# Rows of a third block gathered ahead of a conditional group, x of four chunks added on GpSimd, the second block table moved behind a weighing

## The chip, the cores and the metric

The kernel runs on one core of one Trainium2 chip. The metric is the device time of one execution in microseconds. The timeline and every time below count from the first instruction of the profiled execution of the kernel before.

## The reference

One adaLN transformer block over 4096 tokens of width 256, with linear attention (16 heads of 64) and a mixture of 8 experts of which each token takes two. Everything is float32.

```python
mod = (silu(c) @ wmod).reshape(...)            # sa, ca, ga, sb, cb, gb; |ga|, |gb| at least 0.25
h = layernorm(x) * (1 + ca) + sa
q, k, v = split(h @ w_qkv)                     # 16 heads of 64
q = softmax(q * 64**-0.5, axis=-1)             # over the head's columns
k = softmax(k, axis=-2)                        # over the tokens
ctx = einsum('bhnd,bhne->bhde', q, k)
x = x + ga * (einsum('bhde,bhnd->bhne', ctx, v) @ w_out + b_out)
h = layernorm(x) * (1 + cb) + sb
p = softmax(h @ Wg + bg)                       # 8 experts
sel = p on its two largest, divided by their sum (+1e-8)
e = gelu(h @ W1[e] + b1[e]) @ W2[e] + b2[e]    # hidden width 1024, each expert
x = x + gb * sum_e sel[e] * e
```

## The kernel before

The 4096 tokens are eight chunks of 512, a chunk being four tiles of 128 tokens (`TPC = 4`). Tile `t` of chunk `i` lies in `xs[i][:, t, :]`; `hT[i]` holds the normalized input of the chunk, transposed, in two blocks of 128 features (`KB = 2`).

**First half (0 to 342 us).** Keys, their column maxima, queries, the context and from it one matrix `weff` of 256 by 264, so that attention's output of a tile is two matmuls with the tile's `hT` as weights. The last 8 columns give what attention adds to the router's logits; `raw` holds the part of the logits that comes from x.

**Residual and routing (342 to 404 us).** `residual(i, half, cols)` makes two tiles of a chunk in one PSUM tile `po` of a pool of three. For each tile it issues two matmuls with `weff`, then one matmul with the identity that adds x (256 columns) and one that adds `raw` (8 columns). `products(i)` calls it for both halves; `park(i)` calls `keep`, where ScalarE copies `po` to `xs[i]` and to `logits`. `chunk_stats(i)` takes mean and variance of four tiles on VectorE (`bn_stats`, `bn_aggr`). A `Route` of a chunk makes its expert choice: `distances`, `power` (the exponential, ScalarE), `choose` (VectorE, result `both`), `places` (TensorE, result `pp`), `weigh` and `aim` (VectorE, beginning with the instructions that write `total` and `of_hot`), `mark` (8 one-hot tiles of a chunk on GpSimd and 8 on VectorE, written over parts of `hT` and `weff_t` that are no longer needed), `enlist` (8 matmuls that add the marks to the PSUM tile `listed`). Routes 0 to 3 are chunks 0 to 3; route 4, named `last`, holds chunks 4 to 7.

**Blocks (404 to 935 us).** Tokens are worked on by expert, in blocks of 256 (pairs) or 128 (single) rows of one expert. `early_table` makes the table of five blocks from the first three chunks; `late_table` makes the rest, 23 pairs and 15 singles, and needs the counts `cnt2` of all chunks. A table's `where` gives the row and expert of a block; `name_tokens` turns the lists into token numbers, `who`. For a block, `load_weights` issues two loads of 1 MB and two small ones on SyncE's queue, `load_rows` one indirect gather per 128 rows on GpSimd into one of four `held` buffers, `prepare` transposes the rows on TensorE (`ptb`) and ScalarE copies them to `xT`, `hidden` is 16 matmuls `ph` with a gelu each two, `weights_of` multiplies the gate weights (`g`, `gs`), `project` is 16 matmuls `py` for a pair and 8 for a single, then two VectorE instructions per 128 rows (the weighing, result `y`), and `add_to_out` scatters `y` into the output by GpSimd, adding, one scatter after the other. PSUM pool `ps_b`, three buffers, serves both `ptb` and `py`; `ps_a`, four buffers, serves `ph` and the small products.

`run` goes through blocks: hidden of block s, prepare of block s+1, then project of block s-1. Of eight chosen blocks the routing work is laid between these steps by the dictionary `steps`: `(b, 1)` runs after block b's `weights_of`, `(b, 2)` after the projection of the block ahead of b.

The order on the engines is the order of the calls as far as `InOrder` chains it, up to the end of the first five blocks; beyond, the tile scheduler places TensorE, VectorE, ScalarE and SyncE instructions, and GpSimd stays in call order.

Of the singles, four (`once`) run only if the number of units `left` exceeds 54, three (`twice`) only if it exceeds 58: two `tc.If` groups. In this input the first group runs and the second does not. `middle` is 17: blocks at positions 5 to 16 of `order_of` run, then the group `once`, then positions 17 to 35. In the text a block from position 17 on is called by its position: 17 is a single, 18 and 19 are pairs, 20 a single, 21 a pair. Ahead of a group's end the rows of what follows are gathered by `beyond`:

```python
            if s == len(some) - 2:
                load_ahead(beyond)
...
    run(order_of[EARLY:middle], once[:1], once + order_of[middle : middle + 2])
```

## Time and profile before

| what | us |
|---|---|
| times of 3 runs | 936.43, 936.63, 940.14 (median 936.63) |
| the profiled execution's own time | 936.49 |
| its span, first to last instruction | 934.7 |
| outside the span | 1.8 |
| TensorE matmul busy in the span | 879.8 (94%) |
| VectorE, ScalarE, GpSimd busy | 397.9, 341.6, 377.2 |
| mean granted TensorE clock | 0.977 |

The 94% of TensorE is a share of time in which a matmul is in the pipe, not a share of its peak. A row of the timeline reads: start, duration, engine, line, operation, output <- inputs, count, and in brackets how long the engine stood idle ahead of it and what ended that. A row of the chain of waits reads: start, duration, and what the program's last instruction was waiting for in that time, followed backwards.

### The profile page before, as it was taken

What the parts mean: (1) busy time and instruction counts of PE and PEld (TensorE: products, weight loads), DVE (VectorE), ACT (ScalarE), POOL (GpSimd) and SP (SyncE); (2) the same over time, 40 slices, a digit from 0 to 9 for tenths busy, and PEclk for the clock granted to TensorE, in tenths of its full rate; (3) what the DMA queues carried; (4) which work ended last, traced back from release to release, by engine and by line L of the source; (5) the groups of instructions that cost most, each with busy time, mean ns of one, the idle gap of its engine ahead of it and who ended that gap; (6) DMA issues with size and microseconds to landing.
All of it is one profiled execution on the core that took longest, in us unless ns stands there. A gap on an engine that the chain in (4) does not pass through costs nothing.

```text
span 934.7 us, 13057 instructions
## 1 busy us (share of the span) xinstructions
PE 879.8 (94%) x4747; PEld 661.7 (71%) x4747; DVE 397.9 (43%) x1014; ACT 341.6 (37%) x627; POOL 377.2 (40%) x330
## 2 busy tenths in 40 slices
PE   7979999999999889989799999999859999999996
PEld 4444444455545578878588989988759898898885
DVE  5454453798888838859831111112100111111111
ACT  4314343344444425363223333433324334333330
POOL 2000000478998803348843434342132333333242
PEclk9979999999999999999999999999979999999998
DMA  9000000232000002485878777785947877867622
GB/s 341 5 2 1 1 1 1 63 113 96 1 1 1 1 1 92 146 289 198 288 199 232 186 232 222 211 247 122 353 139 232 248 211 204 257 209 202 175 41 24
DMA packets 85077, 130.52 MB, mean 140 GB/s; under 512 B 11343, under 2 KB 66675, under 8 KB 85012
## 3 DMA queue, kind: packets, MB, share of 16 engines
q1 hardware_dynamic: 71568, 111.98, 36.2%
q0 software_dynamic: 13440, 17.69, 10.1%
q8 instruction: 39, 0.64, 0.3%
q14 instruction: 26, 0.21, 0.1%
q10 hardware_dynamic: 4, 0.00, 0.0%
HBM read 113.23 MB, written 17.47 MB: 140 GB/s over the span
## 4 chain that ended last, share of the span: by engine, by line
PE 74%; DVE 9%; issue 6%; POOL 5%; DMA 4%; ACT 1%; POOLq 0%; SPq 0%; ACTq 0%; DVEq 0%
PE ph L1220 19%; PE py L1241 17%; PE pk L292 12%; PE pq L292 10%; DMA out_dram<-y,who 3%; PE pctx L554 3%; PE po L36 2%; PE ph L36 2%; PE py L36 2%; POOL out_dram L36 1%; DVE hT L36 1%; POOL qs L36 1%; PE pa L367 1%; PE ptb L1193 1%; PE pt L196 1%
## 5 line engine op out<-in xcount | busy, mean ns | idle before, releaser
L1227 ACT ACTIVATE gl<-ph,b_sb 128x256 f32<-128x256 f32 (+1 forms) x280 | 122.2, 437 | 273.0 <-PE ph L1220 266.7
L36 POOL DMA_INDIRECT out_dram<-y,who x68 | 107.3, 1577 | 281.4 <-DVE y L1250 227.7
L1241 PE MATMUL py<-w_sb,gl 128*128 128x256 f32 x960 | 212.8, 379 | 0.0
L1220 PE MATMUL ph<-xT,w_sb 128*128 128x256 f32 (+1 forms) x1120 | 209.5, 346 | 0.5 <-ACT xT L1196 0.5
L1220 PEld LDWEIGHTS ph<-xT,w_sb 128*128 128x128 f32 x1120 | 186.6, 193 | 20.1 <-ACT xT L1196 0.7
L1241 PEld LDWEIGHTS py<-w_sb,gl 128*128 128x128 f32 x960 | 180.1, 190 | 23.1
L292 PE MATMUL pq<-wq,hT 128*128 128x512 f32 x256 | 118.3, 604 | 1.2 <-DVE qs L36 1.2
L292 PE MATMUL pk<-wk,hT 128*128 128x512 f32 x256 | 116.2, 606 | 0.3 <-ACT hT L199 0.3
L1249 DVE SCALAR_TENSOR_TENSOR y<-py,gs,gb_bc 128x256 f32<-128x256 f32 x60 | 29.0, 483 | 163.9 <-PE py L1241 157.4
L1206 DVE TENSOR_TENSOR g<-held,mine 128x16 f32<-128x16 f32 (+1 forms) x31 | 5.3, 172 | 209.4 <-DMA held<-tokens_d,who 209.4
L292 PEld LDWEIGHTS pk<-wk,hT 128*128 128x128 f32 x256 | 48.3, 194 | 60.1 <-issue 55.1
L292 PEld LDWEIGHTS pq<-wq,hT 128*128 128x128 f32 x256 | 46.0, 190 | 49.5 <-issue 45.9
L36 POOL DMA_INDIRECT held<-tokens_d,who x64 | 66.4, 1038 | 26.9 <-issue 17.2
L36 POOL TENSOR_TENSOR qs<-qs,qsum 128x1024 f32<-128x1024 f32 x30 | 58.2, 1941 | 15.6 <-DVE qsum L36 15.6
L36 DVE TENSOR_TENSOR qs<-qs,pk 128x1024 f32<-128x1024 f32 x31 | 37.8, 1220 | 62.3 <-ACT ka L453 44.1
L36 ACT ACTIVATE qs<-qs 128x1024 f32<-128x1024 f32 x32 | 33.8, 1055 | 38.2 <-DVE qs L36 38.2
L453 ACT ACTIVATE ka<-pk 128x1024 f32<-128x1024 f32 x24 | 24.6, 1023 | 57.9 <-PE pk L292 57.9
L498 POOL MEMSET qs<- 128x8 f32 x8 | 0.9, 118 | 110.3 <-PE pt L196 79.2
L36 DVE TENSOR_REDUCE qmax<-pq 128x16 f32<-128x1024 f32 x32 | 38.6, 1206 | 14.0 <-PE pq L292 13.8
L36 POOL TENSOR_TENSOR ka<-ka,nk_bc 128x1024 f32<-128x1024 f32 x18 | 42.6, 2364 | 0.0
L36 POOL TENSOR_SCALAR hT<-upward,slot 128x128 f16<-128x128 f16 x48 | 30.5, 924 | 25.6 <-DVE slot L36 13.3
L36 DVE TENSOR_TENSOR qs<-pq,qmax 128x1024 f32<-128x1024 f32 x32 | 39.2, 1225 | 3.1
(289 smaller groups left out, 995.6 us busy)
## 6 DMA issues: line engine op xcount, KB each, us to landing
w_sb<-in_L_ffn_W_dram SPq DMA_DIRECT2D x80, 1024.0 KB, 6.4
x<-in_L_attn_x_dram SPq DMA_DIRECT2D x16, 512.0 KB, 6.6
b_sb<-b_d SPq DMA_DIRECT2D x40, 128.0 KB, 5.9
tokens_d<-row SPq DMA_DIRECT2D x8, 528.0 KB, 2.9
out_dram<-x SPq DMA_DIRECT2D x8, 512.0 KB, 6.0
ka<-in_L_wmod_dram SPq DMA_DIRECT2D x3, 512.0 KB
out_dram<-y,who POOLq DMA_INDIRECT x68, 5.0
wk<-in_L_attn_w_qkv_dram SPq DMA_DIRECT2D x2, 512.0 KB, 8.1
```

Source lines behind the costliest of these rows:

```text
L36: ins = getattr(self.engine, name)(*args, **kwargs)
L196: on.pe.transpose(pt[:, t * P : (t + 1) * P], src[:, t, kb * P : (kb + 1) * P], ident)
L292: nc.tensor.matmul(pw[:, half * 512 : (half + 1) * 512], hT[i][:, kb, t * P : (t + 1) * P], w[:, kb, half * 512 : (half + 1) * 512], start ...
L367: nc.tensor.matmul(pa[32 * kb : 32 * kb + 32, :], gate_w[:, kb, :], plain(i)[:, kb, :], start=True, stop=True,)
L453: nc.scalar.activation(k_tile(n), pk, AF.Identity)
L554: nc.tensor.matmul(pctx[g][h * DH : (h + 1) * DH, j, :], ek[:, q * P + h * DH : q * P + (h + 1) * DH], qs[:, q, h * HW : (h + 1) * HW], st ...
L1193: on.pe.transpose(pt[:, j * P : (j + 1) * P], xg[:, j, kb * P : (kb + 1) * P], ident)
L1206: on.dve.tensor_tensor(g[:, :nt, :], xg[:, :nt, D : D + E], mine[:, b : b + 1, :].to_broadcast([P, nt, E]), ALU.mult,)
L1220: on.pe.matmul(ph[:, :rows], w1_sb[:, kb, hb * P : (hb + 1) * P], xT[:, kb, :rows], start=(kb == 0), stop=(kb == KB - 1),)
L1227: on.act.activation(gl[:, hb, :rows], ph[:, :rows], AF.Gelu_apprx_tanh, bias=b1_sb[:, hb : hb + 1])
L1241: on.pe.matmul(py, gl[:, hb, j * P : (j + 1) * P], w2_sb[:, hb, :], start=(hb == 0), stop=(hb == HB - 1),)
L1249: on.dve.scalar_tensor_tensor(y, py, gs[:, j : j + 1], gb_bc, ALU.mult, ALU.mult)
```

## The change

Three things. First, for chunks 4 to 7 the two identity matmuls of each tile are gone; ScalarE parks attention's part over the chunk's own `hT`, GpSimd adds it to `xs[i]` in one instruction per chunk (`add`), and one VectorE instruction adds `raw` to the logits of these 16 tiles. Second, between the blocks 1 and 2 of the early five, `late_table` changes place with the marks of chunks 6 and 7: the marks go ahead of the projection of block 1, the table behind it. Third, `beyond` gets one block more (three blocks of the positions 17 to 19 instead of two, and the third single of `twice` one step later than the other two), whose gather is issued in the last step of the group.

```diff
@@ residual
         po = ps_r.tile([P, 2, 512], FP, tag="r", name="po")
+        whole = i <= FIRST
...
-                    stop=False,
-                )
-            on.pe.matmul(po[:, z, :D], ident, xs[i][:, t, :], start=False, stop=(cols == D))
-            if cols > D:
+                    stop=(kb == KB - 1 and not whole),
+                )
+            if whole:
+                on.pe.matmul(po[:, z, :D], ident, xs[i][:, t, :], start=False, stop=(cols == D))
+            if whole and cols > D:
@@ keep
+    def parked(i: int):
+
+        return xs[i] if i <= FIRST else hT[i].rearrange("p kb (z d) -> p (kb z) d", d=D)
+
     def keep(i: int, half: int, po, more: bool = True):
-        on.act.activation(xs[i][:, 2 * half : 2 * half + 2, :], po[:, :, :D], AF.Identity)
+        on.act.activation(parked(i)[:, 2 * half : 2 * half + 2, :], po[:, :, :D], AF.Identity)
...
+    def add(i: int):
+        on.pool.tensor_tensor(xs[i], xs[i], parked(i), ALU.add)
@@ the order of the residual stage
     rows = {b: load_rows(b) for b in range(3)}
+    add(4)
+    add(5)
     for i in (6, 7):
         products(i)
         park(i)
...
     routes[3].begin_rows()
     routes[3].rows_on_pool(0)
     routes[3].choose()
+    add(6)
+    add(7)
+    tiles = slice((FIRST + 1) * TPC, NT)
+    on.dve.tensor_tensor(logits[:, tiles, :], logits[:, tiles, :], raw[:, tiles, :], ALU.add)
     for i in (4, 5, 6):
         chunk_stats(i)
@@ steps
-        (2, 1): [lambda: late.extend(late_table()), lambda: store(3), lambda: store(4)],
+        (2, 1): [
+            lambda: mark_last(2), lambda: mark_last(3), lambda: store(3), lambda: store(4)
+        ],
         (2, 2): [
-            lambda: mark_last(2), lambda: mark_last(3),
-            lambda: last.enlist(0), lambda: last.enlist(1),
+            lambda: late.extend(late_table()), lambda: last.enlist(0), lambda: last.enlist(1)
         ],
@@ run
-            if s == len(some) - 2:
-                load_ahead(beyond)
+            if s >= len(some) - 2:
+                load_ahead(beyond[: len(beyond) - (s == len(some) - 2)])
@@
-    run(order_of[EARLY:middle], once[:1], once + order_of[middle : middle + 2])
+    run(order_of[EARLY:middle], once[:1], once + order_of[middle : middle + 3])
```

## The prediction

> **What bounds the kernel now.** The page first: matmuls are busy for 94% of the span, so time is won only where TensorE stands still or does work that can go away.

> ```profile
> PE 879.8 (94%) x4747; PEld 661.7 (71%) x4747; DVE 397.9 (43%) x1014; ACT 341.6 (37%) x627; POOL 377.2 (40%) x330
> ...
> PE 74%; DVE 9%; issue 6%; POOL 5%; DMA 4%; ACT 1%; POOLq 0%; SPq 0%; ACTq 0%; DVEq 0%
> ```

> The chain of waits says where the other 26% are. The change touches three places of it. The first, from the timeline (start, duration), is the residual stage.

> ```profile
> 389.31 1.14 PE L36 MATMUL po<-weff,hT 128*128 128x264 f32 x4
> 390.29 0.59 PE L36 MATMUL po<-x,ident 128*128 128x256 f32 x2
> 390.72 0.28 PE L36 MATMUL po<-raw,ident 128*128 128x8 f32 x2
> 390.86 1.14 PE L36 MATMUL po<-weff,hT 128*128 128x264 f32 x4
> ...
> 402.58 0.66 PE L36 MATMUL ptb<-ident,held 128*128 128x128 f32 x4 [0.76 <-ACT logits L36]
> ...
> 414.74 0.19 DVE L36 TENSOR_REDUCE total<-prob 128x4 f32<-128x32 f32 x1 [10.36 <-ACT prob L36]
> ```

> A tile takes 1.55 us (390.86 less 389.31), of which 0.98 us, up to the identity matmul, are attention's. Blocks begin at 402.58, when ScalarE has emptied the last tile. At 414.74 VectorE had stood for 10.36 us: from there the chain runs through VectorE (weighing, marks, statistics, choice of the last four chunks).

> Second, the table among the early blocks, TensorE's rows alone.

> ```profile
> 456.37 0.38 PE L36 MATMUL ptb<-ident,held 128*128 128x128 f32 x2
> 459.52 0.44 PE L36 MATMUL ptb<-ident,held 128*128 128x128 f32 x2 [2.76 <-DVE y L36]
> 461.21 2.43 PE L36 MATMUL listed<-hT,hT 128*128 128x256 f16 x8 [1.25 <-DVE hT L36]
> 463.43 7.68 PE L36 MATMUL py<-w_sb,gl 128*128 128x256 f32 x32
> ```

> Block 1's projection was done at 445.7, but VectorE weighed it only behind the table, at 458.99, so its PSUM buffers came free late, and then the marks were late: TensorE lost most of 456.75 to 463.43.

> Third, the chain behind the first conditional group.

> ```profile
> 671.64 2.77 issue
> 674.41 7.42 DMA out_dram<-y,who
> ...
> 685.82 2.81 DMA held<-tokens_d,who
> ...
> 689.36 5.54 PE ph L1220 x32
> ```

> Rows of block 19 are gathered on GpSimd behind the group's last scatter (682.58), which waits for the scatter ahead of it; its transposes stand on TensorE ahead of block 17's hidden layer, so TensorE idles from 675.45 to 687.47. The windows of 1 us add a price (after the length stand five busy times with their counts, PE to POOL, then the granted clock, the DMA share and GB/s).

> ```profile
> 679.00:680.00 1.00, 0.00 (x0) 0.00 (x0) 0.00 (x0) 0.00 (x0) 0.00 (x0) 0.85 0.93 221
> ...
> 692.00:693.00 1.00, 1.00 (x7) 1.00 (x7) 0.35 (x2) 0.51 (x2) 0.00 (x0) 0.50 0.03 8
> 693.00:694.00 1.00, 1.00 (x9) 1.00 (x9) 0.00 (x0) 0.54 (x2) 0.00 (x0) 0.82 0.00 0
> ```

> The clock halves about 4.2 us after the last matmul and is full again about 4 us after dense work resumes: 32 `ph` passes took 5.74 us there against 3.57 us elsewhere, so a closed clock costs 2.2 us.

> **Part 1, residual.** Removed: 16 tiles x 0.57 = 9.1 us of TensorE. Added: four GpSimd adds at 2.36 us (18 adds of two 128x1024 operands, `ka<-ka,nk_bc`, lie between 2.354 and 2.380) = 9.4 us, and one VectorE add of 128x128, 0.28 us (row `far<-logits,rstd`), in a stretch where VectorE has room. ScalarE copies as much as before. What is left on the path: chunk 4's shorter products free `of_hot` of chunk 2, for which VectorE waited 0.91 us, so the early table, `who` and the gathers come 0.9 us earlier, no more, since VectorE is busy from there to 391.6. Chunks 6 and 7 stand behind the table's matmul, which waits for `t_chosen` (388.35, now 387.45); they begin at 387.7 and, 8 tiles at 0.98, end at 395.5; PSUM is free at 396.4 instead of 402.5. The next thing late is block 0's rows: their first gather landed after 7.8 us, neighbours after 6.0 to 6.6, among 6 MB of weights; that gives transposes at 399.6 and, 1.2 us later (as at 411.58 to 412.76), `ph` at 400.8 against 404.55: 3.7 us.

> Then VectorE: behind its choice for chunk 3 stand the statistics of chunks 4 to 6, which now wait for GpSimd, and behind these `weigh` of chunk 3, for which TensorE waits through `of_hot` and GpSimd's marks through `slot`. GpSimd: six gathers to 399.3, adds 4 and 5 to 404.0, four rows of chunk 3 (2.15) to 406.2, add 6 to 408.5; statistics 4 x 0.53 to 410.6, block 0's gate 0.4: 411.0 against 414.74, again 3.7 us. Block 3's gathers, behind add 7, move from 402.5 to 411; they are needed at 434. So both limits say -3.7. An add at the slowest row of this shape, 3.38 us (`x<-x,gab_bc`), would leave -0.6.

> **Part 2, table.** In before's times: VectorE ends chunks 4 and 5's marks and block 2's gate at 441.95, then 16 marks (5.0, as the first 16 took) to 446.95, block 1's weighing (4 x 0.48) to 448.95, and the table. The order in the built program sets two clears of `hT` into its first steps, and they wait for both lists on TensorE, which end at 449.6 as before, GpSimd's marks being late; so the table starts at 450.4. It took 16.95 us with two clears of 0.72; with one in it, 16.2: 466.6. TensorE: block 3's hidden layer ends at 456.5, transposes no longer wait, the list of chunk 6 has its marks (GpSimd's by 456.2), `py` of block 2 starts at 458.1 and ends at 465.2, chunk 7's list and the copies take 2.4 as before, block 4's `ph` starts at 467.5 against 473.34: -5.8. Given back: VectorE weighs block 2 behind the table, to 469.0, then `who`; rows of block 5 landed 6.5 us after `who` began (473.48 to 480.0), so at 475.5, with `ph` done at 474.5: -4.8. SyncE's loads of block 5 wait for `where`, now at about 460 instead of 451.8, and are needed at 482. Bounds: nothing given back, -5.8; table and `who` 2 us later, -2.8.

> **Part 3, the group.** Block 19's gather takes 2 x 1.3 us of GpSimd behind the scatter of 624.91, where it idles 8.97 us to the next at 635.49: free, as its buffer is. The same holds for the third `twice` gather behind the scatters near 907. Then transposes of 17 to 19 end near 676.5, `ph` of 17 (its weights were issued at 657.85) at 680.1, `py` at 683.8. Next late: block 20, whose gather is now first behind the group's last scatter, 684.44 as before. Landing took 2.8 to 5.1 us where I looked, median of all 3.7: 688.1, and block 18's `ph` starts at 688.6 against 698.56: -10.0. Bounds 687.3 and 689.5, so -10.8 to -8.6.

> **The clock** decides the rest. Part 1 leaves TensorE idle from 395.5 to 399.6 and part 3 from 683.8 to 688.1: 4.1 and 4.3 us, at the edge of the 4.2 us seen. Each, if closed, gives back 2.2. I take one closed, one open. [...]

> **Sum.** -3.7 - 4.8 - 10.0 + 2.2 = -16.3. The profiled execution took 936.49 (934.7 and 1.8 outside), the median is 936.63, so 936.5 - 16.3 = 920.2.

> **Rivals.** (a) The group pays nothing: the order on the other engines (VectorE's gate of block 21 stands ahead of block 17's weighing) holds PSUM until rows of 21 are in, 691, and the wait only moves. Against it: TensorE needs that buffer only behind block 18's hidden layer, past 695. Then -3.7 - 4.8 + 2.2: 930.2. Chance 0.10. (b) The table comes so late that part 2 gives nothing: block 5's rows 4.8 us later than I have them. For it: VectorE is full from 436 to 469. 925.0; chance 0.12. (c) Slower: the adds hold up everything. VectorE, at the statistics of chunk 6, has three adds ahead; each us an add costs over 2.36 puts `weigh`, and all blocks, 3 us later. From 2.36 + 16.3 / 3 = 7.8 us an add the kernel is slower than before; at 9 us it takes 940.1. For it: VectorE and GpSimd slow each other in this trace (3.38 against 2.36). Against: no such row is near 7.8. Chance 0.05. (d) The change does not gather ahead: the built program's order on GpSimd shows the gather ahead of the group, so no chance of its own.

> **Numbers.** The forecast has 0.73, of which the case of both gaps open (918.0) and both closed (922.4) are part. Low: 3.7 + 5.8 + 10.8 with the clock open, 916.2. High: 0.6 + 2.8 + 8.6 with both closed, 928.9; this takes in (b), and of (a) half. A measurement tells some 0.5% here: faster is below 931.9, the same up to 941.3. (a) ends just inside faster and spills over: faster 0.89, same 0.06, slower 0.05.

> **What would show it.** Right: matmuls `po` of chunks 6 and 7 at 0.98 us a tile; four adds of 2.4 us on GpSimd; statistics waiting for GpSimd; `total` some 2 to 4 us earlier; no wait of `ptb` for `y` near 456; `py` of block 2 at once behind one list; the gap behind the group of 4 to 5 us instead of 12, ending in the rows of a single; and the granted clock in the two gaps. Wrong: `total` at or after 414.7, a wait of 4 us or more at block 5's rows, or a gap behind the group still above 8 us.

## The result and the profile after

The changed kernel takes 935.25 us (median of 20 runs, 930.57 to 937.95) against 939.13 us (20 runs, 934.98 to 941.62) for the kernel before on the same chips: a ratio of 0.9962, interval 0.9950 to 0.9975. It is 3.9 us faster, within the 0.5% that I had called no change, where 16.3 us were forecast.

The profiled executions differ by more, 931.30 against 936.49, but 1.6 us of that lie ahead of everything the change touches: the first residual matmul begins at 341.89 before and at 340.29 after. In the profiles of this study, whose programs are the same up to there, it begins anywhere from 340.29 to 346.80. So the stage times of the tables below are counted from that matmul; in that count the end moved from 592.8 to 589.1, by 3.7 us. Rows of a profile keep their own time, from the first instruction of that kernel's execution.

| start of the hidden layer (`ph`), from the first residual matmul | before | after | moved by | forecast |
|---|---|---|---|---|
| block 0 | 62.7 | 59.5 | -3.2 | -3.7 |
| block 1 | 70.9 | 70.3 | -0.6 | -3.7 |
| block 4 | 131.5 | 124.7 | -6.8 | -9.5 |
| block 5 | 145.8 | 148.1 | +2.3 | -8.5 |
| position 19, behind the group | 363.9 | 360.3 | -3.6 | -16.3 with the clock |
| end of the span | 592.8 | 589.1 | -3.7 | -16.3 |

Parts 1 and 2 were worth more than nothing at block 4 and less than nothing one block later; all that is left comes from part 3. The page of the changed kernel:

```profile
PE 873.7 (94%) x4683; PEld 654.0 (70%) x4683; DVE 398.6 (43%) x1015; ACT 341.7 (37%) x627; POOL 385.8 (42%) x334
...
PE 17%; issue 5%; DMA 3%; POOL 1%; POOLq 0%
```

The 64 matmuls that are missing are the identity matmuls. (The chain can be followed back only to the group here, so its shares can't be set against those of before.) The residual stage, from the timeline of TensorE, then of GpSimd and VectorE:

```profile
385.90 7.37 PE L36 MATMUL po<-weff,hT 128*128 128x264 f32 x32
397.44 0.30 PE L36 MATMUL ptb<-ident,held 128*128 128x128 f32 x1 [4.18 <-DMA held<-tokens_d,who]
...
399.80 9.78 PE L36 MATMUL ph<-xT,w_sb 128*128 128x256 f32 x32 [0.28 <-ACT xT L36]
```

```profile
397.66 4.66 POOL L36 TENSOR_TENSOR x<-x,hT 128x1024 f32<-128x1024 f32 x2
...
400.05 0.43 DVE L36 BATCH_NORM_STATS2 st<-x 128x6 f32<-128x256 f32 x1 [4.64 <-POOL x L36]
...
406.79 0.43 DVE L36 BATCH_NORM_STATS2 st<-x 128x6 f32<-128x256 f32 x1 [2.21 <-POOL x L36]
...
412.57 0.19 DVE L36 TENSOR_REDUCE total<-prob 128x4 f32<-128x32 f32 x1 [3.26 <-ACT prob L36]
```

Eight residual tiles take 7.37 us, TensorE then idles until block 0's rows are in, and the hidden layer that follows takes 9.78 us instead of 7.20. The adds take 2.33 us each and VectorE waits for them, as forecast, but its statistics are done by 409.0; `total` then waits for ScalarE's exponential, which stands behind the eight gelus of that long hidden layer. Windows of 1 us show why it is long (after the five busy times: granted clock, DMA share, GB/s; a share of about 1 means that the DMA engines are full).

```profile
397.00:398.00 1.00, 0.30 (x1) 0.14 (x1) 0.00 (x0) 0.00 (x0) 0.98 (x2) 1.00 0.99 385
398.00:399.00 1.00, 0.39 (x2) 0.39 (x3) 0.00 (x0) 0.00 (x0) 1.00 (x1) 0.63 1.05 375
404.00:405.00 1.00, 1.00 (x4) 0.81 (x3) 0.54 (x3) 0.09 (x1) 1.00 (x2) 0.50 1.01 408
405.00:406.00 1.00, 1.00 (x6) 0.82 (x5) 0.00 (x0) 0.47 (x1) 1.00 (x1) 0.95 1.06 366
```

The granted clock falls from 1.00 to 0.50 at 398.3 and is back at 405.1. Next the table among the early blocks:

```profile
454.33 0.60 PE L36 MATMUL ptb<-ident,held 128*128 128x128 f32 x4
...
455.64 7.07 PE L36 MATMUL py<-w_sb,gl 128*128 128x256 f32 x32
...
477.50 0.47 PE L36 MATMUL ptb<-ident,held 128*128 128x128 f32 x1 [5.00 <-DMA held<-tokens_d,who]
478.72 0.90 PE L36 MATMUL ptb<-ident,held 128*128 128x128 f32 x3 [0.74 <-DMA held<-tokens_d,who]
479.42 9.14 PE L36 MATMUL py<-w_sb,gl 128*128 128x256 f32 x32
```

The wait of the transposes for `y` is gone and `py` of block 2 starts at once, but 22 us later TensorE waits 5.0 us for the rows of block 5, and `py` of block 4 begins at half clock behind that (granted 0.50 up to 483.6; 9.14 us against 7.07 for block 2). GpSimd's rows there, after and then before, tell where the rows were; the last line of each is how long that first gather of block 5 took from its issue to its landing:

```profile
461.02 1.56 POOL L36 DMA_INDIRECT out_dram<-y,who  x1 [0.30 <-DVE tmp L36]
469.66 1.55 POOL L36 DMA_INDIRECT out_dram<-y,who  x1 [7.08 <-DVE gs L36]
471.52 1.10 POOL L36 DMA_INDIRECT held<-tokens_d,who  x1 [0.30 <-issue]
...
DMA to landing us min/median/max: 5.9/5.9/5.9
```

```profile
463.99 1.55 POOL L36 DMA_INDIRECT out_dram<-y,who  x1 [0.30 <-DVE hT L36]
473.86 1.55 POOL L36 DMA_INDIRECT out_dram<-y,who  x1 [8.31 <-DVE who L36]
475.78 1.09 POOL L36 DMA_INDIRECT held<-tokens_d,who  x1 [0.37 <-DVE who L36]
...
DMA to landing us min/median/max: 3.2/3.2/3.2
```

After the change the token numbers of block 5 were cast at 467.47, but the gather went out at 471.52: ahead of it on GpSimd stands a scatter of block 2, which waits until block 1's has landed (issued at 461.02, landed after 7.8 us). (The row puts the wait down to `gs`, which VectorE finished at 469.0; the test below names the scatter.) Before, the same scatter stood there too, but left at 473.86, while `who` was still being worked out (to 474.99): it cost nothing. The landing itself became longer too: a block's rows are two gathers, and both halves were in 7.2 us after the first was issued (471.52 to 478.72), against 4.2 before (475.78 to 480.0). Behind the group:

```profile
677.01 3.74 PE L1229 MATMUL ph<-xT,w_sb 128*128 128x128 f32 x32
680.58 3.62 PE L1250 MATMUL py<-w_sb,gl 128*128 128x256 f32 x16
690.77 0.66 PE L1202 MATMUL ptb<-ident,held 128*128 128x128 f32 x2 [6.57 <-DMA held<-tokens_d,who]
691.22 9.05 PE L1229 MATMUL ph<-xT,w_sb 128*128 128x256 f32 x32
```

The gap of 12.0 us has become one of 6.6, ending in the rows of the single at position 20, and the hidden layer behind it again begins at half clock (granted 0.50 from 688.4 to 695.2).

### The profile page after: what moved, and what is told of

Its sections match the earlier page's. It is cut to its first block, busy times and chain, and to the rows that moved or that the text cites. A ratio compares the mean times of both kernels' runs of the same rounds, so it can differ in the third digit from the quotient of the medians.

```text
span 929.4 us, 12932 instructions
## 1 busy us (share of the span) xinstructions
PE 873.7 (94%) x4683; PEld 654.0 (70%) x4683; DVE 398.6 (43%) x1015; ACT 341.7 (37%) x627; POOL 385.8 (42%) x334
## 5 line engine op out<-in xcount | busy, mean ns | idle before, releaser
L36 POOL DMA_INDIRECT out_dram<-y,who x68 | 107.4, 1579 | 279.1 <-DVE y L1259 216.0
L36 POOL DMA_INDIRECT held<-tokens_d,who x64 | 66.5, 1039 | 26.8 <-issue 18.7
L36 DVE TENSOR_TENSOR qs<-qs,pk 128x1024 f32<-128x1024 f32 x31 | 37.9, 1221 | 62.3 <-ACT ka L453 44.2
L36 POOL TENSOR_TENSOR qs<-qs,qsum 128x1024 f32<-128x1024 f32 x30 | 58.1, 1937 | 15.6 <-DVE qsum L36 15.6
L36 ACT ACTIVATE qs<-qs 128x1024 f32<-128x1024 f32 x32 | 33.8, 1055 | 38.2 <-DVE qs L36 38.2
L36 DVE TENSOR_REDUCE qmax<-pq 128x16 f32<-128x1024 f32 x32 | 38.6, 1206 | 13.9 <-PE pq L292 13.8
L36 POOL TENSOR_TENSOR ka<-ka,nk_bc 128x1024 f32<-128x1024 f32 x18 | 42.4, 2358 | 0.0
L36 DVE TENSOR_TENSOR qs<-pq,qmax 128x1024 f32<-128x1024 f32 x32 | 39.2, 1225 | 3.1
L36 PE MATMUL ph<-xT,w_sb 128*128 128x256 f32 x160 | 38.9, 402 | 1.4 <-ACT xT L36 0.7
```

The costliest lines, as they stand in the source:

```text
L36: ins = getattr(self.engine, name)(*args, **kwargs)
```

## The experiments

All counts of microseconds in this table are from the first residual matmul of the kernel's own profiled execution; the ratio is that of the times (6 to 20 runs) to the kernel before. The counts come from one execution each and say where time went; what a kernel is worth, the ratio says. The two can differ by some us: experiment 3 ends 4.1 us earlier by its profile, while its times are 0.83% shorter, nearly 8 us.

| kernel | block 1 | block 4 | block 5 | end | ratio (interval) |
|---|---|---|---|---|---|
| before | 70.9 | 131.5 | 145.8 | 592.8 | |
| changed | 70.3 | 124.7 | 148.1 | 589.1 | 0.9962 (0.9950 to 0.9975) |
| 1 residual alone | 70.2 | 131.1 | 145.4 | 592.6 | 0.9999 (0.9974 to 1.0024) |
| 2 table alone | 70.7 | 125.2 | 148.8 | 596.0 | 1.0033 (1.0009 to 1.0057) |
| 3 gather alone | 71.0 | 133.3 | 147.6 | 588.7 | 0.9917 (0.9893 to 0.9942) |
| 4 changed, table undone | 70.2 | 130.6 | 145.1 | 585.9 | 0.9917 (0.9886 to 0.9949) |
| 5 changed, gathers first | 70.2 | 124.7 | 144.6 | 585.7 | 0.9918 (0.9893 to 0.9944) |
| 6 changed, gaps kept busy | 67.5 | 121.8 | 145.1 | 585.7 | 0.9914 (0.9887 to 0.9941) |
| 7 changed, call order behind the group | 70.1 | 124.5 | 147.8 | 580.8 | 0.9868 (0.9841 to 0.9895) |
| 8 changed, fourth block ahead | 70.1 | 124.5 | 148.5 | 581.7 | 0.9862 (0.9831 to 0.9893) |
| 9 as 5, stores later | 70.4 | 124.8 | 145.8 | 586.5 | 0.9936 (0.9914 to 0.9959) |
| 10 residual alone, gap busy | 68.1 | 127.9 | 142.9 | 590.1 | 0.9983 (0.9959 to 1.0006) |
| 11 gathers first, call order, first gap busy | 70.2 | 125.2 | 145.7 | 578.7 | 0.9810 (0.9781 to 0.9839) |
| 12 table undone, call order, first gap busy | 67.3 | 127.9 | 142.2 | 575.1 | 0.9825 (0.9793 to 0.9856) |
| 13 as 5, weights of block 6 held | 70.2 | 124.7 | 141.1 | 582.9 | 0.9890 (0.9861 to 0.9918) |
| 14 as 11, weights of block 6 held | 67.3 | 122.1 | 138.1 | 571.6 | 0.9790 (0.9758 to 0.9821) |

### The three parts, each alone (1 to 4)

Each takes its own lines of the diff and leaves the rest as before; the fourth is the changed kernel with `late_table` and the marks back in their old places.

> Kernel before with the residual part alone. Theory (the clock takes half of it): the hidden layer of block 0 starts 4 to 5 us earlier, behind an idle stretch of about 4 us in which the granted clock closes, so that its 32 matmuls take 9.8 us instead of 7.2, and block 1 starts only about 2.2 us earlier (410.6 against 412.8). Nothing behind it takes this back: the end is 2 us earlier, about 934.5. Rival (the adds hold VectorE up): block 1 starts earlier, but by the hidden layer of block 5 (487.7 before) the gain is gone: 936.5. My forecast's own term, 3.7 us: 932.8.

> Kernel before with the moved table alone. Theory (the gather of block 5 stands behind a scatter on GpSimd): the hidden layer of block 4 starts about 6 us earlier (467 against 473.3), but the rows of block 5 come only 2 to 3 us earlier than before, TensorE waits some 5 us for them, the clock closes, and the hidden layer of block 5 starts 2 to 3 us later than 487.7: the kernel is slower by 2 to 3 us, about 939. Rival (the loss needs the residual part too, since only an early start leaves the rows late): no loss, -1 to -5 us, 932 to 935.5.

> Kernel before with the third block gathered ahead alone. Theory: TensorE's idle time behind the group falls from 12 to about 6.6 us, since the transposes of block 20 stand ahead of block 18's hidden layer and their rows land about 5.7 us after their gather; with the clock closed behind it, the gain is about 6 us: 930.5. My forecast's own term with landing after 3.7 us: 10 us less 2.2 for the clock, 928.7. Rival (the wait only moves): 936.5.

> Changed kernel with the table put back to its old place (residual and gather parts alone). Theory: the moved table costs more than it saves, so this is about 3 us faster than the changed kernel: 2.2 + 5.9 = 8 us under before, about 928.5. Rival (the table does pay as forecast and the others pay less): 3 to 5 us slower than the changed kernel, 934 to 936.

The residual part starts block 0 3.3 us earlier (59.4), loses 2.6 to the clock (its hidden layer takes 9.82 us), and 0.2 is left at the end: less than my theory's 2 us, which had taken the 1.6 us of luck in the first half for part of the gain. The table alone is slower by 0.33%, as expected: it starts block 4 6.3 us earlier and block 5 3.0 later, with the same wait as in the changed kernel.

```profile
480.11 0.47 PE L36 MATMUL ptb<-ident,held 128*128 128x128 f32 x1 [4.91 <-DMA held<-tokens_d,who]
...
482.24 8.22 PE L36 MATMUL py<-w_sb,gl 128*128 128x256 f32 x32
```

The gather alone ends 4.1 us earlier though it enters block 5 1.8 us late (`py` of block 2, behind an idle stretch that it shares with the kernel before, took 9.0 us there against 7.7; in the kernel before the granted clock was 0.50 there from 461.2 to 464.7, so the clock is the likely reason again), so by the profile it is worth 5.9. With -0.2, +3.2 and -5.9 the parts add up to -2.9, near the -3.7 of the whole, and undoing the table is worth 3.2 us by the profile. The rival of a loss that needs both parts has fallen.

### Why block 5's rows are late (5, 9, 13)

The second scatter of a block is declared free of the order to the first, and that takes it out of GpSimd's chain of call order; the built program has block 2's ahead of the gathers, which are called earlier. Experiment 5 ties it behind them:

```diff
+        ahead = on.pool.last
         for j, y in enumerate(ys):
...
+            if b == 2 and done:
+                tc.add_manual_dep(ins.ins, ahead.ins.name, ..., reason="behind the gathers")
```

> Changed kernel; on GpSimd the second scatter of block 2 is ordered behind the gathers of blocks 5 and 6, as the first is already. Theory (that scatter, waiting for block 1's to land, holds the gather): the first gather of block 5 is issued at about 467.8 instead of 471.5, right behind the token numbers, the rows land about 3.7 us earlier (473.8), TensorE waits 1 to 2 us instead of 5.0, the clock stays open, and py of block 4 takes 7.1 instead of 9.1 us: 5 to 6 us faster than the changed kernel, about 925.5. Rival (the rows are late through the loaded DMA engines, not through the queue): the gather is issued earlier but lands at 477 as now: no change, 931.

```profile
476.05 0.33 PE L36 MATMUL ptb<-ident,held 128*128 128x128 f32 x1 [1.85 <-DMA held<-tokens_d,who]
477.56 0.55 PE L36 MATMUL ptb<-ident,held 128*128 128x128 f32 x3 [1.18 <-DMA held<-tokens_d,who]
477.95 8.76 PE L36 MATMUL py<-w_sb,gl 128*128 128x256 f32 x32
```

The gather goes out at 469.96, 0.8 us behind the cast of `who`; counted from the first residual matmul that is 3.2 us earlier. Block 5 starts 3.5 us earlier, not 5 to 6: the wait is 1.85 and 1.18 us instead of 5.0 and 0.7, but the clock closed all the same (granted 0.50 from 479 to 481). The landing had not become shorter: the first half took 6.0 us, against 3.2 before, and both halves were in 7.6 us after the first gather, against 4.2. (The next expectation sets the 6.1 us up to the first transpose, which needs the first half alone, against the 4.2 of both halves; like for like the gap is wider.) Two more kernels ask why. Experiment 9 moves three stores of 512 KB (`store(5)` to `store(7)`) from ahead of block 6's weights to step (4, 1):

> The kernel with the gathers first (second scatter of block 2 behind the gathers), and the stores of the chunks 5 to 7 into the output (three of 512 KB) moved from ahead of block 6's weights to behind block 4's hidden layer. There the rows of block 5 took 6.1 us to land (469.96 to 476.05), against 4.2 in the kernel before, with the DMA engines full. Theory (the rest of the delay is DMA load): less is queued, the rows land after 3.5 to 4.5 us, TensorE hardly waits at block 5, the clock stays open there: 2 to 4 us faster than with the gathers first alone, about 924 to 926 where that ran 928. Rival (6 us is what the landing takes at this point, whatever is queued): no change.

No gain: block 5 at 145.8 instead of 144.6. Block 6's weights (issued at 462.6 and 463.8) had taken the place of the stores, so this did not tell the two theories apart. Experiment 13 holds those weights back too:

```diff
-                if ahead not in weights and ahead not in done:
+                if ahead not in weights and ahead not in done and (b, ahead) != (4, 6):
...
+            if b == 4:
+                mark_d = tc.dram_tile([P, 1], FP, name="mark_d")
+                on.sp.dma_start(mark_d, xT[:, 0, :1])
+                weights[6] = load_weights(6)
```

> The kernel with the gathers first, and block 6's weights (2 MB) not loaded until the rows of block 5 have been transposed and copied (a store of 512 bytes from block 5's xT goes ahead of them on SyncE's queue and waits for it). Moving the chunk stores had left as much queued, since these weights took their place. Theory (the landing is long because weights fill the DMA engines): the rows land 3.5 to 4.5 us after their gather instead of 6.1, about the time when block 4's hidden layer ends; the clock stays open; block 5's hidden layer starts 3 to 5 us earlier than with the gathers first alone (counted from the first residual matmul 140 to 142 against 144.6), and block 6's weights, needed 14 us later, are in time: about 924.5. Rival (6 us whatever is queued): 144.6 again, or later where block 6 then waits for weights.

```profile
479.93 0.87 PE L36 MATMUL ptb<-ident,held 128*128 128x128 f32 x4 [0.40 <-DMA held<-tokens_d,who]
480.63 7.07 PE L36 MATMUL py<-w_sb,gl 128*128 128x256 f32 x32
```

Both halves of the rows, gathered from 475.28 on, are in by 479.93, after 4.7 us instead of 7.6, and the clock stays open (1.00): block 5 starts another 3.5 us earlier, of which 2.8 reach the end by the profile (the intervals of the two ratios overlap). So the queued weights made the landing long. In windows of 1 us the DMA share where the rows land falls here; in the kernel before it was down to 0.24 there (second fence), and in the changed kernel, last fence, it does not fall.

```profile
478.00:479.00 1.00, 1.00 (x7) 0.87 (x6) 0.00 (x0) 0.61 (x2) 0.98 (x1) 1.00 0.99 405
479.00:480.00 1.00, 0.60 (x4) 0.20 (x2) 0.00 (x0) 0.61 (x2) 0.69 (x2) 1.00 0.71 220
480.00:481.00 1.00, 1.00 (x6) 0.79 (x7) 0.34 (x2) 0.36 (x2) 0.69 (x2) 1.00 0.17 68
```

```profile
478.00:479.00 1.00, 1.00 (x6) 0.90 (x5) 0.00 (x0) 0.61 (x2) 0.69 (x2) 1.00 0.24 76
```

```profile
476.00:477.00 1.00, 0.00 (x0) 0.00 (x0) 0.00 (x0) 0.00 (x0) 0.70 (x2) 0.89 1.07 396
```

### The clock (6, 10)

Extra matmuls into an unused PSUM tile, `idle`, fill part of an idle stretch:

```diff
+    idle = ps_r.tile([P, 2, 512], FP, tag="r", name="idle")
+    for _ in range(4):
+        on.pe.matmul(idle[:, 0, :], ident, xs[0]..., start=True, stop=True)   # behind the last residual tile
...
+            if b == 4:
...
+                for _ in range(10):
+                    on.pe.matmul(idle, ident, w2_sb[:, 0, :], start=True, stop=True)   # experiment 6 only
```

> Changed kernel with extra matmuls whose result nobody uses: four of 512 columns behind the last residual tile (about 2.4 us of the idle 4.2 us) and ten of 256 columns ahead of block 5's transposes (about 2.2 us of the idle 5.0 us). Theory (idle TensorE loses its clock): the granted clock stays at 1 in both places, the hidden layer of block 0 takes 7.2 instead of 9.8 us and py of block 4 7.1 instead of 9.1: 4 to 4.7 us faster than the changed kernel, about 926.5. Rival (these rows are slow for another reason, such as loaded DMA engines or late weights): their lengths stay, no change or up to 1 us slower, 931 to 932.

> Kernel before with the residual part alone, and four extra matmuls of 512 columns, whose result nobody uses, behind the last residual tile. Theory (the residual part is worth 3.3 us, of which the clock takes 2.6): counted from the first residual matmul, block 1 starts 3.3 us earlier than before instead of 0.65, and nothing takes it back: 3 us under before, about 934.5. Rival (something else gives it back, since the residual part alone ended level with before): the clock stays open, block 1 starts 3.3 us earlier, but the end is level with before again.

```profile
396.50 3.60 PE L36 MATMUL idle<-x,ident 128*128 128x512 f32 x8
400.93 0.30 PE L36 MATMUL ptb<-ident,held 128*128 128x128 f32 x1 [0.83 <-DMA held<-tokens_d,who]
401.98 0.55 PE L36 MATMUL ptb<-ident,held 128*128 128x128 f32 x3 [0.75 <-DMA held<-tokens_d,who]
403.02 7.20 PE L36 MATMUL ph<-xT,w_sb 128*128 128x256 f32 x32 [0.48 <-ACT xT L36]
```

In the first gap the theory holds: useless work shortens the hidden layer behind it from 9.78 to 7.20 us, with the rows landing no earlier (first transpose 57.2 us behind the first residual matmul in experiment 6 as in the changed kernel) and the clock at 1.00 throughout. With it the residual part keeps 2.7 us to the end by the profile (590.1 against 592.8); by the times, 0.9983, that is not shown, since the interval takes in no gain. In the second place of experiment 6 the filling did not save the clock:

```profile
472.94 4.48 PE L36 MATMUL idle<-w_sb,ident 128*128 128x256 f32 x20
478.75 0.33 PE L36 MATMUL ptb<-ident,held 128*128 128x128 f32 x1 [1.33 <-DMA held<-tokens_d,who]
479.92 0.90 PE L36 MATMUL ptb<-ident,held 128*128 128x128 f32 x3 [0.84 <-DMA held<-tokens_d,who]
480.61 8.39 PE L36 MATMUL py<-w_sb,gl 128*128 128x256 f32 x32
```

```profile
479.00:480.00 1.00, 0.16 (x2) 0.08 (x2) 0.03 (x1) 0.00 (x0) 0.00 (x0) 0.93 1.08 374
480.00:481.00 1.00, 1.00 (x4) 0.95 (x5) 0.31 (x2) 0.51 (x2) 0.00 (x0) 0.50 1.05 402
```

It closed at 479.9, 2.4 us after the last of the dense matmuls, in which two idle stretches of 1.33 and 0.84 us lay.

### The gap behind the group (7, 8)

Behind the group the scheduler, not the call order, places TensorE's work, and it sets the transposes of position 20 ahead of block 18's hidden layer, whose rows and weights are there. Two cures: chain TensorE in call order (7), or gather 20 ahead of the group as well, into the buffer that the last block ahead of the group frees (8).

```diff
+    on.pe = InOrder(tc, nc.tensor)          # 7
     run(order_of[middle:], [], twice)
...
+            if s == len(some) - 1:          # 8
+                load_ahead(fourth)          # order_of[middle + 3 : middle + 4]
```

> Changed kernel with TensorE's instructions behind the group chained in the order of the calls, so that the transposes of block 20 come behind the hidden layers of 18 and 19 instead of ahead of 18's. Theory (the remaining gap is the transposes of block 20 waiting for rows, ahead of work that is ready): the idle 6.6 us goes, and the clock stays open: 8 to 9 us faster than the changed kernel, about 922.5. Rival (something else behind the group is late, weights or PSUM): the wait moves to block 18's hidden layer, no change, 931.

> Changed kernel with the rows of a fourth block (20) gathered ahead of the group too, in the last step before it, behind that block's gate weights. Theory (the same as for the call order, with the other cure): the transposes of 20 find their rows, the idle 6.6 us goes: 7 to 9 us faster than the changed kernel, about 923. Rival (the order moves the next waiting transposes, of block 21, ahead too, or the weights of 18 are late): part of the wait stays, 926 to 930.

```profile
681.41 0.60 PE L36 MATMUL ptb<-ident,held 128*128 128x128 f32 x4
682.50 7.20 PE L36 MATMUL ph<-xT,w_sb 128*128 128x256 f32 x32 [0.50 <-ACT xT L1205]
...
700.34 0.38 PE L36 MATMUL ptb<-ident,held 128*128 128x128 f32 x2
```

In experiment 7 block 18's hidden layer starts at 682.50 with the clock open (1.00 from 674 to 690), and the transposes of 20 come at 700.34 without a wait. The end comes 8.4 us earlier than in the changed kernel, in experiment 8 7.4 us. In experiment 7 neither weights nor PSUM were late there; in experiment 8 `py` behind block 18's hidden layer waited 0.86 us for a `y` of VectorE.

### Together (11, 12, 14)

> Three cures on the changed kernel together: gathers of block 5 first, TensorE in call order behind the group, and the four extra matmuls behind the last residual tile. If the three act apart, counted from the first residual matmul the end comes 3.5 + 8.4 + 2.8 = 14.7 us earlier than in the changed kernel (574.4 against 589.1), about 916.5; if the clock closes elsewhere instead, 920.

> Changed kernel with the table put back to its old place, TensorE in call order behind the group, and the four extra matmuls. Sum of the parts: 3.3 + 8.4 + 2.8 = 14.5 us earlier than the changed kernel from the first residual matmul on (574.6), about 917: level with the three cures that keep the moved table. If moving the table is worth something once its rows come in time, this one is 2 us or more slower than that.

> The three cures and block 6's weights held back. If the rows of block 5 then land in time, 574.4 less 3 to 5 us: 570 to 571.5 from the first residual matmul, about 913; if not, level with the three cures, 916.5.

Experiment 12 (575.1) is where the sum has it by the count. Experiment 11 is 4 us short of its sum by the profile: the rows of block 0 came 2.1 us after the extra matmuls there, the clock closed at 402.9, and its hidden layer took 8.88 us. By the medians, 921.25 and 921.52, the two are level: even with its gathers first, the moved table has gained nothing that these runs can tell. With block 6's weights held back it may pay: experiment 14, 917.53 us, is the fastest kernel of the study, 2.1% under the kernel before (1.8 to 2.4%) and clearly under the changed one, and its end, 571.6, is close to the 570 to 571.5 expected. Against 11 and 12 its interval overlaps, so that the moved table gains there is not shown; by the profile it is 3.5 us ahead of 12.

## Why the prediction was wrong, point by point

- **Part 1.** The removed matmuls, the adds (2.33 us against 2.36), VectorE's wait for them, and block 0's start (-3.2 against -3.7) were right. The step that failed is the clock's: "I take one closed, one open". All three idle stretches closed the clock, this one in all eight kernels that left it idle (for 3.97 to 4.35 us; the hidden layer behind it took 9.61 to 9.88 us instead of 7.20), and as `total` stands behind ScalarE's gelus of that hidden layer, the 2.6 us went into the routing too: 0.6 us was left at block 1. The price of a closing was not well read either: 2.2 us sets a row's length (5.74) against the distance between two rows (3.57); like for like it is 2.0 (5.74 against 3.73), and here it was 2.6.
- **Part 2, TensorE.** Right: from block 1 to block 4 it gained 6.2 us, forecast 5.8.
- **Part 2, given back.** The term that failed most: 1.0 us forecast, 9.1 measured (block 4 to block 5 grew from 14.3 to 23.5 us). I took the 6.5 us from `who` to both halves of the rows over from before; they became 12.8 (465.97 to 478.72). Of the 6.3 us, 3.3 are the scatter that the gather stands behind (cast to gather 4.05 us instead of 0.8) and 3.0 the longer landing among weights (7.2 instead of 4.2). The third idle stretch that this opened, which my sum did not have, closed the clock: 2.1 more. Rival (b) had named this place, and its sign "a wait of 4 us or more at block 5's rows" came true, but not its cause: the table did not come late.
- **Part 3.** The mechanism was right, the size off: landing took 5.7 us (684.93 to 690.64), not 3.7, and the clock closed, 2.0: -10.0 became -5.9. The DMA share was 0.96 and more from 684 to 690, against 0.24 to 0.48 behind the group before (684 to 688), so the load is the likely reason here too; no run tests it at this place. (Block 18's start before is 698.40 by its row, not 698.56, which changes nothing.) That the gap ends in the rows of position 20 was forecast; that they hold up block 18's hidden layer, which needs nothing of them, I had read as given. It is the scheduler's choice, and worth 8 us.
- **The sum.** -0.6 (part 1 with its clock), +2.9 and -5.9 make -3.6; the end moved by 3.7. Part 1 was right up to the clock, parts 2 and 3 up to the next late thing, the rows, and wrong about how late these were.
- Rivals (a) and (c): neither decided. The adds held up no block that these profiles show (`total` waited for ScalarE), and the group paid.

## What to carry to other kernels

When a step is moved earlier, walk down the queue of the engine that serves its result, and ask of each instruction ahead what it waits for: a scatter that had been covered by the late step became the wait once the step was early (4.05 us from cast to gather instead of 0.8). A latency read from the trace holds for the DMA load that it was read in: the rows of block 5 took 7.6 us with block 6's weights queued and 4.7 with these held back. Move the step, and read the load at its new place. The idle stretches of 4.18, 5.00 and 6.57 us on TensorE in the changed kernel all closed the clock on the dense work behind them and cost 2.6, 2.1 and 2.0 us: price such a stretch as closed, unless work can be put into it up to shortly before its end (in experiment 6 the clock stayed at 1.00 with 0.83 us left idle in the first place and closed with 1.33 us in the second); better, look whether the waiting instruction needs to stand ahead of work that is ready.

## What the runs showed of the hardware that was not expected

```profile
476.45:479.86 3.41, 1.29 (x6) 0.65 (x4) 0.00 (x0) 0.00 (x0) 2.24 (x2) 1.00 1.07 379
```

```profile
347.07:350.48 3.41, 3.41 (x26) 3.14 (x27) 2.29 (x13) 2.44 (x6) 0.00 (x0) 1.00 0.00 0
```

The first held some 1.3 us of matmuls (0.97 us of the extra ones, 0.33 of a transpose), so TensorE need not have stood idle all that time for the clock to close. In the second TensorE was busy throughout, mostly with matmuls of 8 columns, and the clock closed at its end, 10.2 us behind the first residual matmul (10.1 in the kernel before); in all sixteen profiles a row of four `po` matmuls that begins 10.9 to 11.5 us behind the first residual matmul takes 2.00 to 2.11 us instead of 1.14. So the busy time of the profile does not tell when the clock closes, and what does was not shown. Of the two gaps that I had put at 4.1 and 4.3 us, one lasted 4.18 and the other 6.57 us, and both closed the clock. The eight closings behind the residual are less than eight proofs, since the gap was nearly the same in all of them (3.97 to 4.35 us).
